# Reordering the loads of a first attention stage: whole-row rotary query weights, eight folding buffers, bias last

## The chip, the core and the metric

The kernel runs on one core of a Trainium2 chip. The metric is the device time of one execution in microseconds (us). Three runs of the kernel before gave 1918.48, 1918.99 and 1919.78 us; the median is 1918.99 us.

## The reference, cut to what matters

The reference is a decoder of two layers on 4 x 256 tokens of width 512, in float32; every sublayer is added to its input and followed by a layer norm. The change touches only the first attention:

```python
q_c = hidden_size @ Wq_c.T + bq_c
q = (q_c @ Wq_up.T + bq_up).reshape(b, s, NH, Q_HEAD).transpose(0, 2, 1, 3)
kv = hidden_size @ Wkv_c.T + bkv_c
kv_nope, kv_rope = (kv[..., :KV_LORA], kv[..., KV_LORA:])
kvu = (kv_nope @ Wkv_up.T + bkv_up).reshape(b, s, NH, QK_NOPE + V_HEAD).transpose(0, 2, 1, 3)
k_nope, v = (kvu[..., :QK_NOPE], kvu[..., QK_NOPE:])
k_rope = jnp.broadcast_to(kv_rope[:, None, :, :], (b, NH, s, QK_ROPE))
scores = jnp.einsum('bhqd,bhkd->bhqk', q, k) / np.sqrt(Q_HEAD)
out = jnp.einsum('bhsv,Hv->bsH', o, Wo) + bo
```

There are 32 heads (NH). A query head has 128 plain numbers and 64 rotary ones; the query is compressed to 192, keys and values to 64. After this come a gated feed-forward layer with integer weights, a second attention and a routed low-rank layer. Those three stages are the same in both kernels.

## The kernel before, in words

One function, `tile_decoder2`, writes all stages, and a tile framework places the instructions on the engines: PE (TensorE), DVE (VectorE), ACT (ScalarE), POOL (GpSimd), SP (SyncE). Each engine works through its own list in order, and semaphores make one wait for another. All loads are issued by SP, in the order of its list. They share eight semaphores in turn, so a load is issued only when the load eight places earlier has landed.

The first attention never builds keys of 128 numbers a head. It multiplies the query weights of a head with the key weights of that head, so that the query can be compared directly with the compressed 64-number key. The product is kept in `wm`, for each head 64 rotary columns followed by 65 folded ones; it has two halves `m`, of 96 and of 97 rows (the 97th row carries the bias).

- **Folding** (L138 to L158): eight groups `g` of four heads. A group needs its query weights `wqn` (loaded by L127 into a ring of three buffers) and the key weights `wkn` (one load, L122). It makes 16 small matmul records (8 for each `m`), and one copy for each `m` takes the result into `wm`: ACT at L156, DVE at L158.
- **Loads within the loop**: at `g == 1` the compression weights `wqc` and `wkvc` and two biases `cb` (L141 to L144), from `g == 4` on one part of the transposed input `xT` a group (L146).
- **Loads after the loop**: the rotary columns straight into `wm` (L159 and L160), the value bias `bv` (L161), value weights `wvl`, input `x`, `rows`, `wo0` and two scale vectors (L162 to L167).
- **Compression** (L174 to L182): for each half `hf` of the tokens, two products with `wqc` give the compressed query `qcT` (evicted by DVE, L179), and one with `wkvc` gives `kT` (DVE, L182). A float32 matmul shows as two records, so these are 8, 8 and 8 records for each half.
- **First queries** (L186 to L199): four units of four records each, `ps_p<-qcT,wm`, evicted by ACT (L196) into `qh`. Then come `beta` (L209) and the transposes of `kT` (L212).
- **Value bias** (L217): one DVE instruction sums `bv` over the heads. In the DVE's list it stands behind the first eviction into `kT` and ahead of the second half's evictions into `qcT`.

The tag "p" of PSUM has two banks, so a third product in flight waits for the eviction of the first. The lines that set the rotary loads and what stands behind them:

```python
wm = l0.tile([RQ2 + 1, 2, NH, LW], F32, name="wm")
...
nc.sync.dma_start(out=wm[:RQ2, 0, :, :DR], in_=a["wqr0"])
nc.sync.dma_start(out=wm[:, 1, :, :DR], in_=a["wqr1"])
nc.sync.dma_start(out=bv, in_=a["bv"])
nc.sync.dma_start(out=wvl, in_=a["wvl"])
nc.sync.dma_start(out=x, in_=a["x"])
nc.sync.dma_start(out=rows, in_=a["rows"])
```

Of the kernel before, what the change touches and what calls it, by code (L numbers as in the profile page):

```python
# [9 lines left out]
F32 = mybir.dt.float32  # L10
# [6 lines left out]
P = 128  # L17
# [4 lines left out]
NH = 32  # L22
GH = 4
NG = NH // GH
DN, DR, DV = 128, 64, 128
RQ, RKV = 192, 64
RQ2 = RQ // 2
# [10 lines left out]
def tile_decoder2(ctx: ExitStack, tc: tile.TileContext, a: dict, out: bass.AP):  # L38
    nc = tc.nc
# [5 lines left out]
    def bank(tag, shape=(P, 512)):  # L45
        return ps.tile(list(shape), F32, tag=tag, name=f"ps_{tag}")
# [6 lines left out]
    def mm(o, pairs):  # L53
        for i, (l, r) in enumerate(pairs):
            nc.tensor.matmul(o, l, r, start=(i == 0), stop=(i == len(pairs) - 1))  # L55
# [7 lines left out]
        out=mask, in_=mask, pattern=[[0, 2], [-1, P]], compare_op=ALU.is_ge,  # L63
# [3 lines left out]
    x = const.tile([P, NT, D], F32, name="x")  # L67
    xT = const.tile([P, DC, N], F32, name="xT")
    rows = const.tile([P, 3, D], F32, name="rows")
    gsc = const.tile([P, NI], F32, name="gsc")  # L70
    usc = const.tile([P, NI], F32, name="usc")
# [45 lines left out]
    NP = NH // 2  # L117
    FP = 4
    LW = DR + RKV + 1
    with tc.tile_pool(name="l0", bufs=1) as l0, tc.tile_pool(name="l0b", bufs=2) as l0b:  # L120
        wkn = l0.tile([P, NH, RKV + 1], F32, name="wkn")
        nc.sync.dma_start(out=wkn, in_=a["wkn"])  # L122
        wm = l0.tile([RQ2 + 1, 2, NH, LW], F32, name="wm")

        def load_qn(g):
            t = l0b.tile([P, GH, RQ + 1], F32, tag="wqn", name="wqn", bufs=3)
            nc.sync.dma_start(out=t, in_=a["wqn"][:, g * GH:(g + 1) * GH, :])  # L127
            return t

        wqc = l0.tile([P, DC, RQ], F32, name="wqc")  # L130
        wkvc = l0.tile([P, DC, DR + RKV], F32, name="wkvc")
        cb = l0.tile([P, 3], F32, name="cb")
        wvl = l0.tile([P, NP, DV], F32, name="wvl")
        bv = l0.tile([P, NH], F32, name="bv")
        wo0 = l0.tile([P, D], F32, name="wo0")


        for g in range(NG):  # L138
            wqn = load_qn(g)
            if g == 1:  # L140
                nc.sync.dma_start(out=wqc, in_=a["wqc"])  # L141
                nc.sync.dma_start(out=wkvc, in_=a["wkvc"])
                nc.sync.dma_start(out=cb[:RQ2, 0:2], in_=a["bqc"])
                nc.sync.dma_start(out=cb[:, 2:3], in_=a["bkvc"])  # L144
            if g >= 4:
                nc.sync.dma_start(out=xT[:, g - 4, :], in_=a["xT"][:, g - 4, :])  # L146
            heads = slice(g * GH, (g + 1) * GH)
            for m in range(2):
                rows_m = RQ2 + m
                pj = bank("p", (P, GH, RKV + 1))  # L150
                for hh in range(GH):
                    mm(pj[:rows_m, hh, :], [
                        (wqn[:, hh, m * RQ2:m * RQ2 + rows_m], wkn[:, g * GH + hh, :])
                    ])
                if m == 0:
                    nc.scalar.copy(wm[:rows_m, m, heads, DR:], pj[:rows_m])  # L156
                else:
                    nc.vector.tensor_copy(wm[:rows_m, m, heads, DR:], pj[:rows_m])  # L158
        nc.sync.dma_start(out=wm[:RQ2, 0, :, :DR], in_=a["wqr0"])  # L159
        nc.sync.dma_start(out=wm[:, 1, :, :DR], in_=a["wqr1"])  # L160
        nc.sync.dma_start(out=bv, in_=a["bv"])  # L161
        nc.sync.dma_start(out=wvl, in_=a["wvl"])  # L162
        nc.sync.dma_start(out=x, in_=a["x"])
        nc.sync.dma_start(out=rows, in_=a["rows"])
        nc.sync.dma_start(out=wo0, in_=a["wo0"])
        nc.sync.dma_start(out=gsc, in_=a["gsc"])
        nc.sync.dma_start(out=usc, in_=a["usc"])  # L167


        qcT = l0.tile([RQ2 + 1, 2, N], F32, name="qcT")  # L170
# [3 lines left out]
        for hf in range(2):  # L174
            cols = bass.ts(hf, 512)
            for m in range(2):
                pj = bank("p")
                mm(pj[:RQ2], [(wqc[:, c, m * RQ2:(m + 1) * RQ2], xT[:, c, cols]) for c in range(DC)])
                nc.vector.tensor_scalar(qcT[:RQ2, m, cols], pj[:RQ2], cb[:RQ2, m:m + 1], None, ALU.add)  # L179
            pj = bank("p")  # L180
# [21 lines left out]
        for t in range(NT):  # L202
            toks = bass.ts(t, P)
            pj = bank("p", (P, NH))
# [110 lines left out]
        for t in range(NT):  # L315
            pj = bank("p")
# [296 lines left out]
```

## Time and profile before

| what | value |
|---|---|
| median of three runs | 1918.99 us |
| the profiled execution, its own time | 1919.41 us |
| its span, first to last instruction | 1917.6 us |
| PE busy, share of the span | 97% |
| mean granted PE clock | 0.991 |
| DMA, mean over the span | 32 GB/s |
| first folding matmul starts | 7.06 us |
| compression starts | 30.74 us |
| first query unit starts | 84.67 us |

Times in the trace count from the first instruction. "<-" after an idle time names what ended it. The 40 slices of the page are some 48 us wide, so that the opening of the kernel is one or two digits; the parts below read it from finer answers of the trace. DMA share is the busy share of the core's 16 DMA engines; it can read over 1, because the times of packets overlap.

### The profile page before, as it was taken

What the parts mean: (1) busy time and instruction counts of PE and PEld (TensorE: products, weight loads), DVE (VectorE), ACT (ScalarE), POOL (GpSimd) and SP (SyncE); (2) the same over time, 40 slices, a digit from 0 to 9 for tenths busy, and PEclk for the clock granted to TensorE, in tenths of its full rate; (3) what the DMA queues carried; (4) which work ended last, traced back from release to release, by engine and by line L of the source; (5) the groups of instructions that cost most, each with busy time, mean ns of one, the idle gap of its engine ahead of it and who ended that gap; (6) DMA issues with size and microseconds to landing.
All of it is one profiled execution on the core that took longest, in us unless ns stands there. A gap on an engine that the chain in (4) does not pass through costs nothing.

```text
span 1917.6 us, 17357 instructions
## 1 busy us (share of the span) xinstructions
PE 1860.6 (97%) x6384; PEld 997.3 (52%) x6384; DVE 773.2 (40%) x2118; ACT 477.6 (25%) x1526; POOL 51.7 (3%) x65
## 2 busy tenths in 40 slices
PE   8399999999999999999999999999999999999998
PEld 5255566666444444455555555555555555555544
DVE  1066676767611132143333333333333333334554
ACT  0044444444200100222222222222222222222223
POOL 0100000000110010000000000000000000000010
PEclk9699999999999999999999999999999999999999
DMA  5200000000531000010011011011010100100000
GB/s 169 99 1 1 1 1 1 1 1 1 191 132 31 0 1 0 22 42 25 1 44 44 1 45 44 2 43 44 23 44 22 44 28 1 44 23 0 6 11 33
DMA packets 20757, 60.62 MB, mean 32 GB/s; under 512 B 8417, under 2 KB 8673, under 8 KB 15937
## 3 DMA queue, kind: packets, MB, share of 16 engines
q1 hardware_dynamic: 20673, 59.52, 9.2%
q8 instruction: 51, 0.84, 0.2%
q14 instruction: 33, 0.27, 0.0%
HBM read 57.41 MB, written 2.10 MB: 31 GB/s over the span
## 4 chain that ended last, share of the span: by engine, by line
PE 94%; another core or an unknown queue 2%; DVE 2%; DMA 1%; POOL 0%; issue 0%; ACT 0%; SPq 0%; ACTq 0%; DVEq 0%
PE ps_p L55 61%; PE ps_s L55 15%; PE ps_o L55 5%; PE ps_o L280 4%; PE ps_t L263 3%; PE ps_o L476 3%; PE ps_t L465 2%; PE ps_o L477 1%; DMA wqn<-in_wqn 1%; PE ps_t L90 1%; POOL x L371 0%; DVE st L77 0%; DVE x L86 0%; DVE y L370 0%
## 5 line engine op out<-in xcount | busy, mean ns | idle before, releaser
L55 PE MATMUL ps_p<-xT,w_wa 128*128 128x512 f32 x512 | 231.1, 592 | 0.9 <-DVE xT L91 0.9
L55 PE MATMUL ps_p<-w_wd,att 128*128 128x512 f32 x512 | 231.2, 592 | 0.0
L55 PE MATMUL ps_p<-xT,w_wb 128*128 128x512 f32 x512 | 230.1, 592 | 0.0
L55 PE MATMUL ps_p<-w_wc,xT 128*128 128x512 f32 x512 | 229.1, 592 | 0.0
L440 DVE TENSOR_TENSOR ps_s<-ps_s,mask 128x256 f32<-128x256 f32 x128 | 55.3, 432 | 310.2 <-PE ps_s L55 310.2
L241 ACT ACTIVATE pr<-ps_s,ebias 128x256 f32<-128x256 f32 x256 | 117.7, 472 | 142.4 <-DVE ebias L236 142.4
L448 ACT ACTIVATE pr<-ps_s,nmx 128x128 f32<-128x128 f32 (+1 forms) x256 | 105.3, 416 | 177.1 <-DVE nmx L444 177.1
L55 PEld LDWEIGHTS ps_p<-w_wc,xT 128*128 128x128 f32 x512 | 95.1, 190 | 97.1 <-issue 95.7
L55 PEld LDWEIGHTS ps_p<-xT,w_wb 128*128 128x128 f32 x512 | 94.9, 190 | 94.4 <-issue 92.8
L55 PEld LDWEIGHTS ps_p<-xT,w_wa 128*128 128x128 f32 x512 | 94.4, 190 | 92.6 <-issue 91.0
L55 PEld LDWEIGHTS ps_p<-w_wd,att 128*128 128x128 f32 x512 | 94.2, 190 | 90.5 <-issue 89.0
L478 ACT COPY att<-ps_o 128x256 f32<-128x256 f32 x128 | 47.6, 372 | 347.1 <-PE ps_o L477 343.0
L55 PE MATMUL ps_s<-kT,qh 128*128 128x256 f32 x512 | 132.5, 392 | 0.0
L55 PE MATMUL ps_p<-qcT,wm 96*128 96x512 f32 (+1 forms) x256 | 124.6, 599 | 0.0
L55 PEld LDWEIGHTS ps_s<-kT,qh 128*128 128x128 f32 x512 | 88.7, 190 | 35.2 <-ACT pr L241 21.2
L55 PE MATMUL ps_s<-kn,qn 128*128 128x128 f32 (+1 forms) x512 | 105.0, 328 | 0.0
L230 DVE TENSOR_REDUCE nmx<-ps_s 128x2 f32<-128x512 f32 x128 | 88.1, 689 | 36.9 <-PE ps_s L55 36.8
L467 DVE COPY pT<-ps_t 128x384 f32<-128x384 f32 x128 | 70.7, 552 | 50.7 <-PE ps_t L465 50.7
L403 DVE COPY kn<-ps_p 128x512 f32<-128x512 f32 x64 | 44.3, 692 | 108.0 <-PE ps_p L55 108.0
L267 DVE COPY pT<-ps_t 128x512 f32<-128x512 f32 x128 | 86.6, 684 | 0.0
L280 PE MATMUL ps_o<-pT,cN 128*64 128x256 f32 x512 | 83.1, 394 | 0.0
L465 PEld LDWEIGHTS ps_t<-ident,pr 128*128 128x128 f32 x384 | 49.7, 140 | 63.8 <-issue 61.5
(108 smaller groups left out, 2015.0 us busy)
## 6 DMA issues: line engine op xcount, KB each, us to landing
w_wa<-in_wq SPq DMA_DIRECT2D x8, 1024.0 KB, 4.9
w_wb<-in_wk SPq DMA_DIRECT2D x8, 1024.0 KB, 4.9
w_wc<-in_wv SPq DMA_DIRECT2D x8, 1024.0 KB, 4.8
w_wd<-in_wo SPq DMA_DIRECT2D x8, 1024.0 KB, 5.1
wqn<-in_wqn SPq DMA_DIRECT2D x8, 386.0 KB, 4.6
wiwg<-in_wg SPq DMA_DIRECT2D x10, 256.0 KB, 3.5
wiwu<-in_wu SPq DMA_DIRECT2D x10, 256.0 KB, 4.0
wiwd<-in_wd SPq DMA_DIRECT2D x10, 256.0 KB, 5.0
```

Source lines behind the costliest of these rows:

```text
L55: nc.tensor.matmul(o, l, r, start=(i == 0), stop=(i == len(pairs) - 1))
L230: nc.vector.tensor_reduce(nmx[:, i, :], sc, AX.X, ALU.max, negate=True)
L241: nc.scalar.activation(pr[:, i, qt, :], sc[:, qt, :], AF.Exp, bias=bias[:, i, qt:qt + 1], accum_out=sm[:, i, qt:qt + 1],)
L263: nc.tensor.transpose(tp[:, kt, qt * P:(qt + 1) * P], pr[:, i, qt, kt * P:(kt + 1) * P], ident)
L267: nc.vector.tensor_copy(pT, tp)
L280: nc.tensor.matmul(po[i * RKV:(i + 1) * RKV, :], cN[:, 2 * b + kt, :], pTs[i][:, kt, :], start=(kt == 0), stop=(kt == 1),)
L440: nc.vector.tensor_tensor(diag, diag, mask, ALU.add)
L448: nc.scalar.activation(pr[:, pt, :], sc[:, pt, :], AF.Exp, bias=nmx[:, qt:qt + 1], accum_out=sm[:, qt:qt + 1],)
L465: nc.tensor.transpose(tp[:, j, :], pr[:, j, :], ident)
L467: nc.vector.tensor_copy(pT, tp)
L476: nc.tensor.matmul(po, v[g][:, 2 * b, hv], pT[:, 0:2, :], start=True, stop=False)
L478: nc.scalar.copy(att[g][:, hh, b * S:(b + 1) * S], po)
```

## The change

The rotary rows are loaded into a buffer of their own, `wqr`, of the layout of their source (8192 bytes for each row), and copied into `wm` on chip, in four copies for each half: ACT for the 96 rows, POOL for the 97. `wkn` is cut into eight loads, one a group, and both `wkn` and `wqn` get eight buffers, so that no load waits for a matmul. All loads are issued ahead of the folding loop, in a new order: four groups, `wqc` and its biases, then a part of `xT` and a group in turn, `wkvc`, the rotary rows, `wvl`, `x`, `rows`, `bv`, `wo0` and the scales. The buffers of the folding (`l0m`) are given back after the copies, and the later buffers (`l0b`) are placed where they lay.

```diff
-    with tc.tile_pool(name="l0", bufs=1) as l0, tc.tile_pool(name="l0b", bufs=2) as l0b:
-        wkn = l0.tile([P, NH, RKV + 1], F32, name="wkn")
-        nc.sync.dma_start(out=wkn, in_=a["wkn"])
+    with ExitStack() as st0:
+        l0 = st0.enter_context(tc.tile_pool(name="l0", bufs=1))
         wm = l0.tile([RQ2 + 1, 2, NH, LW], F32, name="wm")
-        def load_qn(g):
-            t = l0b.tile([P, GH, RQ + 1], F32, tag="wqn", name="wqn", bufs=3)
-            nc.sync.dma_start(out=t, in_=a["wqn"][:, g * GH:(g + 1) * GH, :])
-            return t
...
-        for g in range(NG):
-            wqn = load_qn(g)
-            if g == 1:
-                nc.sync.dma_start(out=wqc, in_=a["wqc"])
-                nc.sync.dma_start(out=wkvc, in_=a["wkvc"])
-                nc.sync.dma_start(out=cb[:RQ2, 0:2], in_=a["bqc"])
-                nc.sync.dma_start(out=cb[:, 2:3], in_=a["bkvc"])
-            if g >= 4:
-                nc.sync.dma_start(out=xT[:, g - 4, :], in_=a["xT"][:, g - 4, :])
...
-        nc.sync.dma_start(out=wm[:RQ2, 0, :, :DR], in_=a["wqr0"])
-        nc.sync.dma_start(out=wm[:, 1, :, :DR], in_=a["wqr1"])
-        nc.sync.dma_start(out=bv, in_=a["bv"])
-        nc.sync.dma_start(out=wvl, in_=a["wvl"])
-        nc.sync.dma_start(out=x, in_=a["x"])
-        nc.sync.dma_start(out=rows, in_=a["rows"])
...
+        with tc.tile_pool(name="l0m", bufs=1) as l0m:
+            wkn = [l0m.tile([P, GH, RKV + 1], F32, name=f"wkn{g}") for g in range(NG)]
+            wqn = [l0m.tile([P, GH, RQ + 1], F32, name=f"wqn{g}") for g in range(NG)]
+            wqr = l0m.tile([RQ2 + 1, 2, NH, DR], F32, name="wqr")
+
+            def load_group(g):
+                heads = slice(g * GH, (g + 1) * GH)
+                nc.sync.dma_start(out=wkn[g], in_=a["wkn"][:, heads, :])
+                nc.sync.dma_start(out=wqn[g], in_=a["wqn"][:, heads, :])
...
+            for g in range(4):
+                load_group(g)
+            nc.sync.dma_start(out=wqc, in_=a["wqc"])
+            nc.sync.dma_start(out=cb[:RQ2, 0:2], in_=a["bqc"])
+            nc.sync.dma_start(out=cb[:, 2:3], in_=a["bkvc"])
+            for g in range(4, NG):
+                load_xT(g - 4)
+                load_group(g)
+            nc.sync.dma_start(out=wkvc, in_=a["wkvc"])
+            nc.sync.dma_start(out=wqr[:RQ2, 0], in_=a["wqr0"])
+            nc.sync.dma_start(out=wqr[:, 1], in_=a["wqr1"])
+            nc.sync.dma_start(out=wvl, in_=a["wvl"])
+            nc.sync.dma_start(out=x, in_=a["x"])
+            nc.sync.dma_start(out=rows, in_=a["rows"])
+            nc.sync.dma_start(out=bv, in_=a["bv"])
+            nc.sync.dma_start(out=wo0, in_=a["wo0"])
...
+            for h0 in range(0, NH, NH // 4):
+                heads = slice(h0, h0 + NH // 4)
+                nc.scalar.copy(wm[:RQ2, 0, heads, :DR], wqr[:RQ2, 0, heads, :])
+                nc.gpsimd.tensor_copy(wm[:, 1, heads, :DR], wqr[:, 1, heads, :])
+        l0b = st0.enter_context(tc.tile_pool(name="l0b", bufs=2))
```

In the built program the list of PE is the same, instruction by instruction. DVE's differs in one place: the sum of `bv` now stands behind both evictions into `qcT` of the second half and ahead of the second eviction into `kT`. ACT and POOL have four copies more. SP issues 33 loads instead of 26 for this stage. From the feed-forward layer on, every list is the same, and the first load there waits for the same DVE and PE instructions as before.

More of the change, by code (lines that the diff above doesn't have):

```diff
@@ L135, in tile_decoder2 @@
         wo0 = l0.tile([P, D], F32, name="wo0")
-        for g in range(NG):
-            wqn = load_qn(g)
-            if g == 1:
-                nc.sync.dma_start(out=wqc, in_=a["wqc"])
-                nc.sync.dma_start(out=wkvc, in_=a["wkvc"])
-                nc.sync.dma_start(out=cb[:RQ2, 0:2], in_=a["bqc"])
-                nc.sync.dma_start(out=cb[:, 2:3], in_=a["bkvc"])
-            if g >= 4:
-                nc.sync.dma_start(out=xT[:, g - 4, :], in_=a["xT"][:, g - 4, :])
[L147 to L158, printed above, removed]
@@ L159, in tile_decoder2, with load_xT @@
-        nc.sync.dma_start(out=wm[:RQ2, 0, :, :DR], in_=a["wqr0"])
-        nc.sync.dma_start(out=wm[:, 1, :, :DR], in_=a["wqr1"])
-        nc.sync.dma_start(out=bv, in_=a["bv"])
-        nc.sync.dma_start(out=wvl, in_=a["wvl"])
-        nc.sync.dma_start(out=x, in_=a["x"])
-        nc.sync.dma_start(out=rows, in_=a["rows"])
-        nc.sync.dma_start(out=wo0, in_=a["wo0"])
-        nc.sync.dma_start(out=gsc, in_=a["gsc"])
-        nc.sync.dma_start(out=usc, in_=a["usc"])
+        with tc.tile_pool(name="l0m", bufs=1) as l0m:
[6 more added lines that the diff above has]
+                nc.sync.dma_start(out=wqn[g], in_=a["wqn"][:, heads, :])
+            def load_xT(c):
+                nc.sync.dma_start(out=xT[:, c, :], in_=a["xT"][:, c, :])
+            for g in range(4):
[14 more added lines that the diff above has]
+            nc.sync.dma_start(out=wo0, in_=a["wo0"])
+            nc.sync.dma_start(out=gsc, in_=a["gsc"])
+            nc.sync.dma_start(out=usc, in_=a["usc"])
+            for g in range(NG):
+                heads = slice(g * GH, (g + 1) * GH)
+                for m in range(2):
+                    rows_m = RQ2 + m
+                    pj = bank("p", (P, GH, RKV + 1))
+                    for hh in range(GH):
+                        mm(pj[:rows_m, hh, :], [
+                            (wqn[g][:, hh, m * RQ2:m * RQ2 + rows_m], wkn[g][:, hh, :])
+                        ])
+                    if m == 0:
+                        nc.scalar.copy(wm[:rows_m, m, heads, DR:], pj[:rows_m])
+                    else:
+                        nc.vector.tensor_copy(wm[:rows_m, m, heads, DR:], pj[:rows_m])
+            for h0 in range(0, NH, NH // 4):
+                heads = slice(h0, h0 + NH // 4)
+                nc.scalar.copy(wm[:RQ2, 0, heads, :DR], wqr[:RQ2, 0, heads, :])
+                nc.gpsimd.tensor_copy(wm[:, 1, heads, :DR], wqr[:, 1, heads, :])
```

## The prediction

> **What bounds the kernel now.** The page gives PE 97% of the span, so only the time in which PE stands still can be won cheaply. I read the chain of waits from the start first, to find where the chain leaves PE.
>
> ```profile
> 21.05 6.95 DMA wqn<-in_wqn
> 27.99 0.14 issue
> 28.13 14.05 PE ps_p L55 x40
> 42.18 0.02 issue
> 42.20 0.75 DVE kT L182
> 42.95 34.65 another core or an unknown queue
> 77.61 0.02 issue
> 77.63 0.19 DVE bvs L217
> ```
>
> From 42.95 to 77.61 the chain is on nothing that computes: 34.65 us end in DVE's sum of the value bias. So I read the timeline there.
>
> ```profile
> 22.67 4.59 SPq L160 DMA_DIRECT2D wm<-in_wqr  x1
> ...
> 27.30 47.95 SPq L161 DMA_DIRECT2D bv<-in_bv  x1
> ...
> 75.31 0.42 SPq L162 DMA_DIRECT2D wvl<-in_wvl  x1
> ...
> 77.63 0.19 DVE L217 TENSOR_REDUCE bvs<-bv 128x1 f32<-128x32 f32 x1 [34.68 <-DMA bv<-in_bv]
> 77.73 1.39 DVE L179 TENSOR_SCALAR qcT<-ps_p,cb 96x512 f32<-96x512 f32 x2
> ...
> 78.53 6.31 PE L55 MATMUL ps_p<-xT,wkvc 128*128 128x512 f32 x8 [29.49 <-DVE qcT L179]
> ...
> 84.67 7.04 PE L55 MATMUL ps_p<-qcT,wm 96*128 96x512 f32 x16
> ```
>
> SP spends 47.95 us on issuing the 16 KB of `bv`: it can't hand it over, because the load before it, the 97 rotary rows (L160), is still being cut up. DVE works in order, so both evictions of `qcT` stand behind the sum, and PE, with two PSUM banks full, stands still for 29.49 us. Then the busy time by stretch:
>
> ```profile
> 36.00:50.00 14.00, 13.03 (x31) 4.94 (x29) 1.58 (x3) 0.00 (x0) 0.00 (x0) 1.00 0.08 17
> 50.00:74.00 24.00, 0.00 (x0) 0.00 (x0) 0.00 (x0) 0.00 (x0) 0.00 (x0) 0.56 0.08 17
> ...
> 78.00:79.00 1.00, 0.47 (x1) 0.48 (x2) 1.00 (x2) 0.00 (x0) 0.00 (x0) 0.50 1.07 434
> 79.00:80.00 1.00, 1.00 (x2) 0.36 (x2) 0.13 (x1) 0.00 (x0) 0.00 (x0) 0.50 1.15 442
> ...
> 83.00:84.00 1.00, 1.00 (x3) 0.48 (x2) 0.00 (x0) 0.00 (x0) 0.00 (x0) 0.59 1.11 475
> 84.00:85.00 1.00, 1.00 (x3) 0.39 (x3) 0.12 (x1) 0.00 (x0) 0.00 (x0) 1.00 0.80 340
> ```
>
> The last three columns are the granted PE clock, the DMA share and GB/s. While PE waits, the core moves only 17 GB/s at a share of 0.08, that is 1.3 engines of 16 (packet times overlap, so I read one). When the wait is over, the loads run at 434 to 475 GB/s. The L160 load is the slow one. It has 97 x 32 = 3104 pieces of 256 bytes, 795 KB, and 795 KB at 17 GB/s are 46.8 us: the whole stall.
>
> **What the Trainium skill says.** "DMA: Bandwidth & Descriptors", section "Why a DMA increments its semaphore by 16 and not by 1": a transfer uses k engines, the largest k up to 16 that divides the slowest dimension on both sides; 128 or 96 partitions give 16, 127 give 1. 97 is prime, so k = 1. The trace agrees: 0.08 of 16 engines, 17 GB/s. Nothing in the change alters the 97. Same page, "Queues, rings and completion order": each engine takes its pieces in ring order. Then a later load of 16 engines is finished only when its share on the engine with the long queue is. The trace fits (`bv` lands 2.3 us after its hand-over), but doesn't prove it. Same page, "Why small descriptors are slow (HBM only)": some 3 cycles extra for each packet, 27% at 256 bytes. So longer rows help, but don't give 16 engines. "TensorE: Matmul & The Clock Gate", Part 1: half clock after idling, full after some 3.4 us of work; the trace has 5.3 us at half clock (78.53 to 83.8), which I use.
>
> **The change part by part.**
>
> *Start.* Group 0 now needs 528 KB (`wkn` part 133, `wqn` 395) instead of 1460. From 3 to 9 us the loads of before run at 358 to 416 GB/s, mean 392. The 932 KB less are 2.4 us: PE starts at 4.7 instead of 7.06.
>
> *Folding.* Eight groups of 2.6 us (96 records took 15.6 us), plus the 0.5 us wait for L158 as before: 21.3 us, ending at 26.0 instead of 30.7. The waits for `wqn` (1.94 us on PE before 28.13) go, for data come at 1.4 us a group at first and 2.7 us with `xT` between: group 7 needs 6.7 MB, 3 + (6.7 - 0.27)/0.392 = 19.4 us, plus 1 us to land, and PE wants it at 23.4. The extra 7 issues at 0.43 us are 3 us of SP; up to L154 it has 25 issues of about 0.47 us, 12 us in 22. Rows of `wkn` of 1040 instead of 8320 bytes I cost at nothing to 1 us; group 7's 3 us of room cover it.
>
> *Compression.* Same 48 records: from 30.74 to 49.03, and 3.43 for the last eight at full clock, 21.7 us. It ends at 47.7. All of `xT` and `wkvc` have landed by 22.
>
> *Rotary loads.* 7.77 MB stand ahead of the 97 rows: 3 + (7.77 - 0.27)/0.392 = 22.1 us; I take 22.5. Then 795 KB on one engine. Rows of 8192 bytes on one engine alone are not in the trace. Upper bound of the speed: the share of one engine of the full rate, mean 433 GB/s from 78 to 84 us, 27.0 GB/s, 29.4 us. Lower bound: 17 GB/s, as with the 256-byte pieces, 46.8 us. I take 27.0, since the runs of `x`, `wvl` and `rows` at that rate are 6 to 16 KB long. So the 97 rows are through at 51.9 and land at 52.9.
>
> *Copies.* ACT: four of 96 x 512, some 0.6 us each (L196, 598 ns), from about 25 us; ACT has nothing else until the first queries, so they cost nothing. POOL: four of 97 x 512. The nearest row is POOL's 128 x 512 cast, 507 to 885 ns, 613 in the middle: 2.5 us, to 55.4. Behind them on POOL wait the eight additions into `x`, wanted only by the end of attention at 489 us: nothing. PE's first unit waits for the first copy (53.6), ACT's first `qh` for all four (55.4), since `qh` lies where the folding buffers lay. If this were last, PE would go on from 53.6.
>
> *Bias last.* It is not last. `bv` is issued behind `wvl`, `x` and `rows`. On the one engine their shares (64 + 128 + 48 KiB, 246 KB in all) come behind the 795: 246/27.0 = 9.1 us, so `bv` is through at 61.0 and lands at 62.0. DVE meets the sum before the second eviction of `kT`, and behind that eviction waits PE's second query unit for its bank. So: 62.0 + 0.2 (sum) + 0.75 (`kT`, L182) + 0.05 = 63.0. PE stands still from 47.7 to 63.0 but for the first unit. The waiting for the rotary copies (55.4) is hidden behind it by 7.6 us; if that cover went, rival 2 shows what they cost.
>
> *Sum.* Before, the second unit starts at 84.67 + 7.04/4 = 86.4 at full clock. After: 63.0, with 5.3 us at half clock, 2.65 lost: as good as 65.7. The gain is 86.4 - 65.7 = 20.7 us. Every list behind is the same, and PE is the chain from there on. Against the profiled execution (span 1917.6, its own time 1919.41, 1.8 around it) this is 1898.7; the median of the runs shown is 0.4 lower: **1898.3 us**.
>
> **Rivals.**
>
> 1. *The rows spread over 16 engines after all* (the changed form of the load is cut otherwise). Then all is there by 36 us, and the first unit starts at 47.7 instead of 84.67: 37.0 us, 1882 us. Against it: 97 rows on both sides, as before. 0.08.
> 2. *`bv` isn't held by the one engine's queue.* Then the POOL copies are last: PE goes on from 53.6 instead of 85.5 (the middle of the first unit), less 2.65: 29.2 us, 1889.8 us. For it: the trace of before can't tell queueing from the late issue. 0.10.
> 3. *One engine gives 17 GB/s whatever the rows.* Place: the same queue. 1041 KB at 17.0 are 61.2 us: `bv` lands at 22.5 + 61.2 + 1 = 84.7, PE goes on at 85.7, as good as 88.4, 2.0 us later than before: 1921.0 us, slower, because `bv` now has 246 KB ahead of it. It decides below 1041/(86.4 - 2.65 - 1.0 - 1.0 - 22.5) = 17.6 GB/s. For it: 17 is the only one-engine rate in the trace. Against it: the 433 GB/s of 16. 0.07.
>
> **How the numbers follow.** My forecast has 0.75. Its own bounds: at 22 GB/s the queue takes 47.3 us, 8.8 more, with a start 1 us later 1908; with faster loads and copies some 1895. The range takes in rival 2 and leaves out 1 and 3 (0.15): 1888 to 1909. A measurement of this kernel can tell some 0.2% (3.8 us) from no change. Rival 3 at 17 GB/s falls within it, at 16.4 beyond it. Faster 0.93, same 0.05, slower 0.02.
>
> **What would show it.** First folding matmul at 4.7 us, compression from 26, no wait for `wqn`; about 27 GB/s at a share near 0.07 from some 33 us to 61; the sum of `bv` at 62 as DVE's last wait, and ahead of it PE idle for some 15 us; POOL's copies from 53. Wrong: no lone-engine stretch (rival 1); `bv` long there when POOL copies (2); 17 GB/s again (3).

## The result, and the profile after

The changed kernel takes 1908.11 us (four runs, 1907.80 to 1908.18) where the kernel before takes 1919.38 beside it: ratio 0.9941, 95% interval 0.9924 to 0.9959. A second set on another occasion gave 1905.62 against 1919.46, ratio 0.9929 (0.9913 to 0.9946). So by these medians it is 11 to 14 us faster; 1898.3 had been forecast, with 1888 to 1909 as the range.

The chain of waits after still leaves PE once for long, and still for the bias. First column the start, second the length, in us, the longest pieces only:

```profile
18.42 11.79 SPq L155
30.73 9.87 SPq L157
40.64 28.64 DMA bv<-in_bv
69.49 0.67 DVE kT L194
70.21 8.78 PE ps_p L55 x16
```

The chain is on SP and on `bv` until 69.3, and from 70.21 on PE, where it stays through the first queries and the first softmax. The timeline after, of the same instructions as before:

```profile
16.79 0.33 SPq L153 DMA_DIRECT2D wqr<-in_wqr  x1
...
18.08 0.29 SPq L154 DMA_DIRECT2D wqr<-in_wqr  x1
18.42 11.79 SPq L155 DMA_DIRECT2D wvl<-in_wvl  x1
...
27.04 2.18 ACT L177 COPY wm<-wqr 96x512 f32<-96x512 f32 x4 [1.06 <-DMA wqr<-in_wqr]
...
48.20 1.02 PE L55 MATMUL ps_p<-qcT,wm 96*128 96x512 f32 x2
...
59.90 2.29 POOL L178 COPY wm<-wqr 97x512 f32<-97x512 f32 x4 [58.02 <-DMA wqr<-in_wqr]
...
60.57 2.08 PE L55 MATMUL ps_p<-qcT,wm 97*128 97x512 f32 x2 [11.35 <-POOL wm L178]
...
69.31 0.18 DVE L229 TENSOR_REDUCE bvs<-bv 128x1 f32<-128x32 f32 x1 [23.60 <-DMA bv<-in_bv]
...
70.21 8.40 PE L55 MATMUL ps_p<-qcT,wm 96*128 96x512 f32 x12 [7.57 <-DVE kT L194]
```

PE stands still twice, 11.35 us for POOL's copy of the 97 rows and 7.57 us for the eviction behind the bias. The 96 rows had landed at 27.04, the 97 rows at 59.90. The busy time by stretch of that wait (last three columns: granted PE clock, DMA share, GB/s):

```profile
56.00:60.00 4.00, 0.00 (x0) 0.00 (x0) 0.00 (x0) 0.00 (x0) 0.10 (x1) 0.50 0.06 25
60.00:64.00 4.00, 2.08 (x2) 0.50 (x2) 0.00 (x0) 0.60 (x1) 2.19 (x4) 0.50 0.07 29
64.00:68.00 4.00, 0.00 (x0) 0.00 (x0) 0.00 (x0) 0.00 (x0) 0.00 (x0) 0.50 0.06 26
```

One engine in sixteen is a share of 0.0625: a lone engine is at work, at 25 to 29 GB/s where it had 17. The order in which loads land tells who waits behind whom. By their issue and their times to landing, `wvl` lands at 62.3, `x` at 67.2, `rows` at 69.1 and `bv` at 69.3. The gaps after the 97 rows, 2.4, 4.9 and 1.9 us, are the shares of one engine of these loads (65.5, 131 and 49 KB, a sixteenth of each) at 26 to 27 GB/s.

### The profile page after: what moved, and what is told of

Read it like the earlier page. It is cut to its first block, busy times and chain, and to the rows that moved or that the text cites. A ratio compares the mean times of both kernels' runs of the same rounds, so it can differ in the third digit from the quotient of the medians.

```text
span 1906.4 us, 17373 instructions
## 1 busy us (share of the span) xinstructions
PE 1863.8 (98%) x6384; PEld 998.1 (52%) x6384; DVE 773.2 (41%) x2118; ACT 480.4 (25%) x1530; POOL 53.9 (3%) x69
## 4 chain that ended last, share of the span: by engine, by line
PE 93%; DMA 2%; DVE 2%; SPq 1%; POOL 0%; issue 0%; ACT 0%; ACTq 0%; DVEq 0%
PE ps_p L55 59%; PE ps_s L55 15%; PE ps_o L55 5%; PE ps_o L292 4%; PE ps_t L275 3%; PE ps_o L488 3%; PE ps_t L477 2%; DMA bv<-in_bv 2%; PE ps_o L489 1%; SPq L155 1%; PE ps_t L90 1%; SPq L157 1%; POOL x L383 0%; DMA wqc<-in_wqc 0%; DVE st L77 0%
## 5 line engine op out<-in xcount | busy, mean ns | idle before, releaser
L55 PE MATMUL ps_p<-qcT,wm 96*128 96x512 f32 (+1 forms) x256 | 129.1, 617 | 18.9 <-POOL wm L178 11.3
L490 ACT COPY att<-ps_o 128x256 f32<-128x256 f32 x128 | 47.7, 372 | 346.7 <-PE ps_o L489 342.7
```

What stands on the lines that cost most here:

```text
L490: nc.scalar.copy(att[g][:, hh, b * S:(b + 1) * S], po)
```

## The experiments

Each time is a median with the kernel before run beside it, 1919.35 to 1919.46 us.

**The bias early.** In the changed kernel the load of `bv` moves ahead of the rotary loads.

```diff
+            nc.sync.dma_start(out=bv, in_=a["bv"])
             nc.sync.dma_start(out=wqr[:RQ2, 0], in_=a["wqr0"])
             nc.sync.dma_start(out=wqr[:, 1], in_=a["wqr1"])
...
-            nc.sync.dma_start(out=bv, in_=a["bv"])
```

> The changed kernel with one load moved: bv is issued ahead of both rotary loads instead of behind rows. Queue theory (the 97 rows lie on one DMA engine and the bias waits behind them and behind its share of wvl, x and rows): bv lands before 30 us, DVE's sum no longer waits, and PE stands still only until POOL's first copy at about 60.5, as in the changed kernel; its second query unit starts at about 62.3 instead of 70.2, so about 7.9 us faster than the changed kernel, 1900 us. Rival theory (the place of the bias doesn't matter, the rotary rows set the end anyway): within 2 us of the changed kernel's 1908.

Measured: 1900.43 us (ratio 0.9901, 0.9887 to 0.9916). The sum of `bv` stands at 27.15 us, and the second wait is gone; the first is not. The timeline of this run:

```profile
60.81 2.29 POOL L178 COPY wm<-wqr 97x512 f32<-97x512 f32 x4 [58.93 <-DMA wqr<-in_wqr]
...
61.48 8.92 PE L55 MATMUL ps_p<-qcT,wm 97*128 97x512 f32 x14 [11.91 <-POOL wm L178]
```

The late bias costs the changed kernel 5 to 8 us (against 1905.62 and 1908.11). The queue theory of the expectation holds.

**97 rows cut into 96 and 1.** In the changed kernel:

```diff
-            nc.sync.dma_start(out=wqr[:, 1], in_=a["wqr1"])
+            nc.sync.dma_start(out=wqr[:RQ2, 1], in_=a["wqr1"][:RQ2])
+            nc.sync.dma_start(out=wqr[RQ2:RQ2 + 1, 1], in_=a["wqr1"][RQ2:RQ2 + 1])
```

> The changed kernel with the load of 97 rows cut in two, 96 rows and 1 row. Queue theory: 96 rows spread over 16 engines, the rotary rows land before 30 us, bv before 40, and PE never stops between the folding and the first queries; the second query unit starts at about 49.9 at full clock instead of 70.2 at half clock: 23 us faster than the changed kernel, 1885 us. Rival theory (what is slow is the amount or the length of the rows, not their number): no change, 1908 us.

Measured: 1882.89 us (ratio 0.9812, 0.9797 to 0.9826), the fastest of all. The chain of waits of this run:

```profile
5.46 2.83 PE ps_p L55 x16
8.31 0.44 DVE wm L175
8.79 46.82 PE ps_p L55 x180
55.62 0.24 PE ps_t L225 x2
```

PE works from 8.79 us to the end of the first queries without a stop. The same bytes in the same order, in loads of 96 rows and one, have landed at 29.26 us: the number of rows was what held the load on one engine, as the rule for k of the Trainium skill ("DMA: Bandwidth & Descriptors", the section named in the prediction) says.

**The kernel before, with that cut alone.** Its pieces stay 256 bytes long, its order and buffers stay.

```diff
-        nc.sync.dma_start(out=wm[:, 1, :, :DR], in_=a["wqr1"])
+        nc.sync.dma_start(out=wm[:RQ2, 1, :, :DR], in_=a["wqr1"][:RQ2])
+        nc.sync.dma_start(out=wm[RQ2:RQ2 + 1, 1, :, :DR], in_=a["wqr1"][RQ2:RQ2 + 1])
```

> The kernel before with only its load of 97 rows cut in two, 96 rows and 1 row, still in 256-byte pieces straight into wm. Queue theory: 3072 pieces over 16 engines take about 3 us, bv is issued and lands before DVE reaches its sum at 43, PE goes on from 49, the first query unit starts at about 52.5 instead of 84.7: 32 us faster than before, 1887 us, better than the changed kernel. Rival theory (the 256-byte pieces are what is slow): within 5 us of before, 1914 to 1919 us.

Measured: 1886.30 us (ratio 0.9827, 0.9813 to 0.9842). One line of the kernel before, cut in two, brings 33 us, more than twice the whole change.

```profile
21.89 0.76 SPq L159 DMA_DIRECT2D wm<-in_wqr  x1
...
22.69 6.22 SPq L160 DMA_DIRECT2D wm<-in_wqr  x1
...
28.95 4.46 SPq L161 DMA_DIRECT2D wm<-in_wqr  x1
...
33.46 0.58 SPq L162 DMA_DIRECT2D bv<-in_bv  x1
...
51.59 7.04 PE L55 MATMUL ps_p<-qcT,wm 96*128 96x512 f32 x16
```

The hand-over of `bv` takes 0.58 us in place of 47.95. The short pieces are not what made it slow. The framework also put DVE's sum of `bv` two evictions later in this run (at 49.02). That is not where the gain comes from: `bv` has landed by 36.4, before the sum's old place behind `kT` (42.2). And a later place with the 97 rows uncut, as in the next run, leaves PE waiting for the rotary rows themselves.

**The order alone.** The changed kernel without its whole rows: the rotary weights go straight into `wm`, and the copies go.

```diff
-            nc.sync.dma_start(out=wqr[:RQ2, 0], in_=a["wqr0"])
-            nc.sync.dma_start(out=wqr[:, 1], in_=a["wqr1"])
+            nc.sync.dma_start(out=wm[:RQ2, 0, :, :DR], in_=a["wqr0"])
+            nc.sync.dma_start(out=wm[:, 1, :, :DR], in_=a["wqr1"])
...
-            for h0 in range(0, NH, NH // 4):
-                heads = slice(h0, h0 + NH // 4)
-                nc.scalar.copy(wm[:RQ2, 0, heads, :DR], wqr[:RQ2, 0, heads, :])
-                nc.gpsimd.tensor_copy(wm[:, 1, heads, :DR], wqr[:, 1, heads, :])
```

> The changed kernel without its whole rows: the new order and the eight buffers are kept, but the rotary weights go straight into wm in 256-byte pieces as before, and there are no copies. Queue theory: the one engine takes 46.8 us from about 25 on, to 72, then 9 us for its share of wvl, x and rows, so bv lands at about 82 and PE goes on at 83: within 3 us of before, 1916 to 1921 us. Rival theory (the early start and the buffers bring the gain): about as fast as the changed kernel, 1908 us.

Measured: 1912.27 us (ratio 0.9964, 0.9952 to 0.9977), between the two theories' figures: faster than the one allows, slower than the other. The times of the loads are as the queue theory has them:

```profile
23.38 47.48 SPq L154 DMA_DIRECT2D wvl<-in_wvl  x1
...
73.27 9.21 PE L55 MATMUL ps_p<-qcT,wm 97*128 97x512 f32 x14 [24.46 <-DMA wm<-in_wqr]
...
82.63 0.19 DVE L224 TENSOR_REDUCE bvs<-bv 128x1 f32<-128x32 f32 x1 [33.89 <-DMA bv<-in_bv]
```

But the framework had put DVE's sum elsewhere: behind the second eviction into `kT`, where PE's query units don't stand behind it. So PE went on at 73.27, when the rotary rows landed, and not at 83. That was left out of the expectation, and it means that this run tells the worth of whole rows only roughly: 4 to 7 us.

**Whole rows alone.** The kernel before, with `wqr` and the copies, its own order and buffers.

```diff
+        wqr = l0.tile([RQ2 + 1, 2, NH, DR], F32, name="wqr")
...
-        nc.sync.dma_start(out=wm[:RQ2, 0, :, :DR], in_=a["wqr0"])
-        nc.sync.dma_start(out=wm[:, 1, :, :DR], in_=a["wqr1"])
+        nc.sync.dma_start(out=wqr[:RQ2, 0], in_=a["wqr0"])
+        nc.sync.dma_start(out=wqr[:, 1], in_=a["wqr1"])
...
+        for h0 in range(0, NH, NH // 4):
+            heads = slice(h0, h0 + NH // 4)
+            nc.scalar.copy(wm[:RQ2, 0, heads, :DR], wqr[:RQ2, 0, heads, :])
+            nc.gpsimd.tensor_copy(wm[:, 1, heads, :DR], wqr[:, 1, heads, :])
```

> The kernel before with whole rows alone: its order of loads and its buffers are kept (bv directly behind the rotary rows), but the rotary weights go in whole rows into a buffer of their own and are copied into wm by ACT and POOL as in the changed kernel. Queue theory: the one engine starts on the 97 rows at about 29 us, takes some 34, and bv lands right behind them at 63 to 64 instead of 77.6: 13 to 15 us faster than before, 1904 to 1906 us, so a little faster than the changed kernel, because nothing else is ahead of the bias. Rival theory (the order and the early loads are needed for the gain): well above the changed kernel's 1908, 1913 or more.

Measured: 1909.95 us (ratio 0.9951, 0.9936 to 0.9966), 4 to 6 us more than expected, so neither theory's figure. The bias landed when it should, at 64.1; again DVE's list was another.

```profile
64.18 0.19 DVE L222 TENSOR_REDUCE bvs<-bv 128x1 f32<-128x32 f32 x1 [26.60 <-DMA bv<-in_bv]
...
65.08 5.32 PE L55 MATMUL ps_p<-xT,wqc 128*96 128x512 f32 x8 [21.42 <-DVE kT L187]
...
73.67 7.04 PE L55 MATMUL ps_p<-qcT,wm 96*128 96x512 f32 x16
```

The sum stands one eviction earlier, so PE stopped with 16 records of the compression still to do instead of 8. It went on 13.5 us earlier than before, but its first query unit started only 11.0 us earlier (73.67 against 84.67).

**The 97 rows last.** In the changed kernel their load goes behind all others of the stage.

```diff
-            nc.sync.dma_start(out=wqr[:, 1], in_=a["wqr1"])
...
             nc.sync.dma_start(out=usc, in_=a["usc"])
+            nc.sync.dma_start(out=wqr[:, 1], in_=a["wqr1"])
```

> The changed kernel with the load of the 97 rows issued last, behind the scales. All other loads of the stage (11.7 MB) are through by about 37 us and bv waits for nothing; then the 97 rows run with nothing beside them. If one engine alone gives 25.5 GB/s and loses speed only beside other loads: 31 us, landing at 68.7, PE's first unit goes on at 69.5, 1909 us. If it gives 23.4 GB/s (the mean that the changed kernel shows from start to landing) whatever runs beside it: landing at 71 to 72, 1911 us. If it gives 27.0: landing at 67, 1907 us.

Measured: 1902.66 us (ratio 0.9913, 0.9896 to 0.9929), better than expected and than the changed kernel. The last of the other loads land at 36.5 to 37.3 us, and the 97 rows 28 to 29 us later:

```profile
65.45 2.29 POOL L178 COPY wm<-wqr 97x512 f32<-97x512 f32 x4 [19.18 <-DMA wqr<-in_wqr]
```

The stretches of this run in which they run alone:

```profile
40.00:44.00 4.00, 4.00 (x10) 1.47 (x9) 0.84 (x2) 0.00 (x0) 4.00 (x5) 1.00 0.06 27
44.00:48.00 4.00, 4.00 (x11) 1.69 (x10) 0.75 (x1) 0.00 (x0) 2.27 (x2) 1.00 0.06 27
48.00:52.00 4.00, 1.85 (x5) 0.54 (x3) 0.75 (x1) 0.00 (x0) 0.00 (x0) 1.00 0.06 27
```

Alone, one engine gives the 27.0 GB/s of the prediction. The time can't be read as the worth of this alone: POOL's additions into `x`, too, were over by 46.3 us, long before the first softmax, and this profile has no half clock at the start of the second attention (both are told below).

**Order and buffers with the cut, but no whole rows.** As "the order alone", with the load into `wm` cut into 96 rows and 1.

> The changed kernel with its order and buffers, but the rotary weights straight into wm in 256-byte pieces, as 96, 96 and 1 rows, and no copies. Queue theory: once no load is on one engine, short pieces cost only some 2 us of a transfer that is hidden, so it is as fast as the whole rows cut the same way, about 1885 us. Rival theory (whole rows are worth something by themselves): more than 4 us slower than that.

Measured: 1883.19 us (ratio 0.9813, 0.9799 to 0.9828), the same as with whole rows (1882.89). Without a lone engine the whole rows and their copies are worth nothing that can be measured.

**The 97 rows with nothing beside them.** The bias early, and `wvl`, `x` and `rows` held back until POOL has copied. Of the loads behind the 97 rows, only `wo0` (256 KB) and the two scales still go out beside them.

```diff
+            nc.sync.dma_start(out=bv, in_=a["bv"])
             nc.sync.dma_start(out=wqr[:RQ2, 0], in_=a["wqr0"])
             nc.sync.dma_start(out=wqr[:, 1], in_=a["wqr1"])
-            nc.sync.dma_start(out=wvl, in_=a["wvl"])
-            nc.sync.dma_start(out=x, in_=a["x"])
-            nc.sync.dma_start(out=rows, in_=a["rows"])
-            nc.sync.dma_start(out=bv, in_=a["bv"])
...
+            for first in (wvl[:RQ2 + 1, 0, 0:1], x[:RQ2 + 1, 0, 0:1], rows[:RQ2 + 1, 0, 0:1]):
+                nc.gpsimd.tensor_copy(first, wm[:, 1, NH - 1, 0:1])
+            nc.sync.dma_start(out=wvl, in_=a["wvl"])
+            nc.sync.dma_start(out=x, in_=a["x"])
+            nc.sync.dma_start(out=rows, in_=a["rows"])
```

> The changed kernel with the bias ahead of the rotary loads, and wvl, x and rows held back until POOL's copies are done (three POOL copies of one column each, out of wm into the first column of wvl, x and rows, make their loads wait). So the 97 rows stand where they do with the bias early, directly behind the 96 rows, but no other large load runs beside them. Beside-theory (one engine is slowed while the other fifteen move wvl, x and rows): the 97 rows land 29 us after the 96, as they did when they were issued last, not 33.4: at about 56.5 instead of 60.8, and the kernel is 4 us faster than with the bias early, 1896 us. Place-theory (the time is lost at the start of the transfer, behind the 96 rows): 33 us again, 1900 us.

Measured: the 97 rows land 29.3 us after the 96 rows, as the beside-theory has it:

```profile
25.99 2.18 ACT L171 COPY wm<-wqr 96x512 f32<-96x512 f32 x4 [0.49 <-DMA wqr<-in_wqr]
...
55.32 2.30 POOL L172 COPY wm<-wqr 97x512 f32<-97x512 f32 x4 [53.44 <-DMA wqr<-in_wqr]
```

PE goes on at 55.99, 5.5 us earlier than with the bias early. But the time is 1899.03 us (ratio 0.9896, 0.9881 to 0.9911), only 1.4 better than with the bias early, and in its profiled execution (1901.99 us, the slowest of its four) the lead is gone before 90 us. The same matmuls, behind the first softmax, with the bias early and then here:

```profile
88.69 1.02 PE L55 MATMUL ps_p<-qcT,wm 97*128 97x512 f32 x2
```

```profile
89.55 1.02 PE L55 MATMUL ps_p<-qcT,wm 97*128 97x512 f32 x2
```

The gain went to a new neighbour. POOL's additions into `x` run from 69.66 to 79.6, as late as with the bias early (70.12 to 80.0), but the first softmax has moved forward and now lies beside them. DVE's timeline in this run:

```profile
71.28 0.88 DVE L248 TENSOR_TENSOR nmb<-nmx,beta 128x4 f32<-128x4 f32 x1
72.19 1.19 DVE L250 TENSOR_TENSOR ebias<-nmb,beta 128x4 f32<-128x4 f32 x1
...
74.88 2.35 DVE L266 TENSOR_SCALAR pr<-pr,rc 128x256 f32<-128x256 f32 x2 [0.24 <-DVE rc L264]
...
77.34 2.43 DVE L266 TENSOR_SCALAR pr<-pr,rc 128x256 f32<-128x256 f32 x2
```

A pair of these scalings takes 0.62 us with the bias early, and 2.4 here. PE waits for them, and then runs at half clock: from 83 to 86 us its granted clock is 0.50, and 1.00 with the bias early.

**The changed kernel again.**

> The changed kernel again, unchanged. In its first profile the gain over the kernel before was 13.0 us up to the last sublayer norm before the second attention, and then 1.7 us went, as the first w_wa matmuls behind that norm ran at half clock. If the half clock comes with this kernel, it is there again. If it is chance from execution to execution, it may be missing, and then the profile's span is about 1904.7 us instead of 1906.4.

Measured: 1905.62 us, and the half clock was missing. The same group in the timeline of the first profile of the changed kernel, and then of this one:

```profile
738.34 5.37 PE L55 MATMUL ps_p<-xT,w_wa 128*128 128x512 f32 x8 [0.88 <-DVE xT L91]
```

```profile
737.35 3.67 PE L55 MATMUL ps_p<-xT,w_wa 128*128 128x512 f32 x8 [0.87 <-DVE xT L91]
```

The granted clock from 738 to 741 us is 0.57 in the first and 1.00 in the second. So 1.7 us come and go with the same program (one execution of the second set, 1907.23 us, has the mean clock of the first set's four, 0.992, and the other three have 0.994); the other 1.0 us between the two spans (1906.4 and 1903.7) is there at the end of the query units (78.45 and 77.41). By its longest matmul (1057 to 1101 ns, against 667), this group was slow in the profiles of the changed kernel's first run, the bias early, the cut of the kernel before, whole rows alone, the cut without whole rows and the 97 rows with nothing beside; in the other five it was not. Differences under 2 us between two of these kernels are not read here.

## Why the prediction was right, and where it was off

The direction held, and the mechanism was the forecast one: the 97 rows stay on one engine, the bias queues behind them, PE's second unit waits for it. The range held only just: 1908.11 is 0.9 us inside its upper end, and the gain is little over half, to two thirds, of the 20.7 us forecast. That end was reckoned from 22 GB/s and a start 1 us later; what came was 24 GB/s for the 97 rows and a start 3.5 us later. That the two came to nearly the same sum is luck.

Two stretches ahead of the 97 rows bear on the first term that was off (last column GB/s):

```profile
21.00:24.00 3.00, 3.00 (x21) 3.00 (x21) 0.43 (x1) 0.37 (x1) 0.00 (x0) 1.00 1.00 231
24.00:27.00 3.00, 3.00 (x19) 3.00 (x19) 0.51 (x2) 0.37 (x1) 0.00 (x0) 1.00 0.23 66
```

By the steps:

- **Start, folding, compression:** 5.17, 26.68 and 48.20 us for 4.7, 26.0 and 47.7. Right within 0.7 us. No wait for `wqn` is left after the first.
- **The sixteen-engine loads ahead of the 97 rows** were mis-sized. They were to be through at 22.5 and land at about 23.5; the 96 rows landed at 27.04, 3.5 us later. The mean of 392 GB/s did not hold to the end: from 21 to 24 us the core moved 231 GB/s, from 24 to 27 only 66. Why the tail is thin, no run tells.
- **The 97 rows** were mis-sized too: 29.4 us forecast, 32.9 from the landing of the 96 rows to their own. The speed of one engine, 27.0, was right for an engine alone: 28 to 29 us when they were last, 29.3 when the others were held back. With `wvl`, `x` and `rows` moving beside them it is 32.9, 33.4 with the bias early, 33.1 with whole rows alone. The prediction put this slowing at nothing, though it had those loads run beside. That other loads slow the engine is shown; by what means is not.
- **The queue behind:** 9.1 us forecast, 9.4 measured. **Copies:** 616 ns each on POOL (2.29 us for four), 614 on ACT, both as assumed; ACT's are hidden.
- **PE goes on** at 70.21 instead of 63.0: the two terms, 3.5 and 3.5, and 0.2. The half clock after the wait took 3.1 us (8.40 for 12 records, which take 5.28) instead of 2.65. So the gain at the end of the query units is 91.56 - 78.45 = 13.1 us and not 20.7; of that the first profile lost 1.7 at the second attention's start, the second did not.

Rival 1's time, 1882, is what the cut into 96 and 1 gives (1882.89): its price was right, and the change left it on the table. Rival 2 falls, since `bv` was held; and where its premise is made true (the bias early) the time is 1900.43 and not 1889.8, mainly because the 97 rows land some 8 us later than it had them. Rival 3 falls: whole rows give 24 GB/s beside other loads and 27 alone, not 17.

What the parts of the change are worth once the 97 rows are cut: the cut alone, which the change doesn't have, is 33.1 us. Order and buffers on top of it are some 3 (1886.30 to 1883.19; the intervals of the two ratios overlap, but the query units end at 55.56 instead of 58.47), and whole rows on top of those nothing. Only while the one engine holds everything up are whole rows worth their copies: they cut its 46.7 us (17 GB/s) to 33.

## What to carry to other kernels

When a stretch shows one sixteenth of the DMA share, look at the number of rows of the load before asking about row lengths or order: 97 rows cost 33 us here, and 96 + 1 cost nothing. A small load that an in-order engine waits for belongs ahead of any such transfer; and where the framework places the instruction that waits can be worth as much as where the load stands (PE went on at 73.27 and not at about 83 in the run of the order alone). When a wait goes, look at what the moved work now runs beside.

## What the runs showed of the hardware that was not expected

- One DMA engine's transfer of 795 KB took 28 to 29.3 us alone, and 32.9 to 33.4 us while the other fifteen moved their shares of 3.9 MB.
- SP's hand-over blocks with few pieces as well: behind 97 pieces of 8 KB, `wvl` took 11.8 us and `rows` 9.9 to hand over, though neither waited for a semaphore then. With the 97 rows last, both took 0.33. With whole rows alone, `bv` was handed over in 0.38 us directly behind the 97 rows, and the load after it, `wvl`, took 15.8. So it is not shown that SP is still cutting the load up, as the prediction has it; what holds SP stays open.
- DVE's scaling of 128 x 256 numbers, source and target in SBUF, took up to 1348 ns beside POOL's additions, and at most 354 with the bias early, where the additions were over. A pair took 2.4 us, about as long as two of the additions (1.28 us each). The two small DVE operations ahead of them (`nmb` and `ebias`, two inputs in SBUF) took 0.88 and 1.19 us, and 0.16 and 0.17 with the 97 rows last. The Trainium skill, "SBUF — State Buffer", section "Who interferes with whom", agrees: DVE and POOL share a port pair, DVE uses it when it has two inputs in SBUF or in a mode that a scaling can run in, and then the second to come waits until the other's instruction is done. That the scalings ran in such a mode, no run shows.
- PE ran at half clock after the same gaps of under 1 us in some executions and not in others of the same program: 5.37 or 3.67 us for eight matmuls, at a granted clock of 0.57 or 1.00.
